# Five edits at the seams between the stages of a graph layer on one core

## The chip, the cores and the metric

The kernel runs on one core of one Trainium2 chip. The metric is the device time of one execution in microseconds (us), as the median of several runs. Engines are called as the profile calls them: PE (TensorE, with PEld for its weight loads), DVE (VectorE), ACT (ScalarE), POOL (GpSimd) and SP (SyncE, which here only issues DMAs).

## The reference

One layer works on 32 graphs of 512 nodes with 256 channels, in float32. In short, with the parts that the kernel's stages answer to:

```python
h = jnp.maximum(_layernorm(x), 0.0)                    # x is (32, 512, 256)
# two convolutions along the nodes, 1 tap and 17 taps, with folded batch norms
c = relu(bn1(conv1d(h^T, conv1_w)))
x_conv = relu(bn2(conv1d(c, conv2_w, pad=8)) + h^T)^T
# message passing with affinities from a 3-wide embedding
s = h @ w_se.T + b_se
A = exp(-dist(s, s)) * adj                              # (32, 512, 512)
msg = relu(h @ w_msg.T + b_msg)
x_nmp = A @ msg
# a GRU cell on [x_conv, x_nmp] and h
gi = concat([x_conv, x_nmp]) @ w_ih.T + b_ih
gh = h @ w_hh.T + b_hh
r, z = sigmoid(gi_r + gh_r), sigmoid(gi_z + gh_z)
n = tanh(gi_n + r * gh_n)
return x + (1 - z) * n + z * h
```

## The kernel before

The 32 graphs go in two groups of 16 (`GB = 16`). Within a group the index `b` below counts from 0 to 15 of that group unless a graph number is given.

**First part** (`first_part`, once per group, L1163). For each graph: `statistics` (mean and variance on DVE, L392 to L397, the power -1/2 on POOL, L398), `normalise` (L400: one instruction for each of the four chunks of 128 nodes, on DVE at L411 or on ACT at L409; the ACT form needs `shift`, which DVE makes at L405), `transpose_h` (eight PE transposes at L419 into two banks, a relu out of each bank at L423, or at L421 on ACT for the second half of the first graph), `conv1` (16 matmuls at L439, an addition on DVE at L442 and a relu on ACT at L443) and `windows_to_freq` (matmuls at L454, copies on ACT at L457), which turns windows of 64 nodes into 80 frequency rows. The 17-tap convolution is later a product per frequency.

In the first group the 17-tap weights are turned into frequency rows beside this: 32 steps of `weights_to_freq` (four matmuls into four banks at L363, four copies out at L371 on DVE and L373 on ACT, and after every second step four DMAs on the SP queue at L377 to a DRAM buffer `wd`). The inner function `between(b)` says how many steps a graph gets: two at b = 0, none at b = 1, then two each, with a third at b = 6 and at b = 11. It also starts other loads, and at b = 6 the step `vectors`, whose POOL instructions (L255 to L267) wait for a DMA. The taps of the next eight input channels come by `load_taps` on the POOL queue at even b (L350, L351).

**Left-over products.** The first group's last four frequency products (`u0` to `u3`, of 40 "units") are done inside the second group's first part. The list `left` (L1440) says at which of five points (`fill`) which of them is prepared (`prepare`: a sum of weights at L470 and a sum of factors at L483, both on POOL) and multiplied (`product`: matmuls at L503, copies at L509 and L510 on ACT, additions at L511 and L512 on DVE). The third entry also holds `*combine.pop(0)`, the load of the gate weights `w_hh` by four DMAs on the POOL queue (L211).

**Nodes** (`nodes`, once per group, L1318). Messages (`message`: matmuls at L558, additions at L560 and L561 on DVE, squares at L564 and relu at L565 on ACT), embedding rows (`features`, L572 to L575), factors (`factors`: two transposes at L580 and L584, a copy at L582 and four masked copies at L587 on ACT), exponents (matmuls at L604, exp on ACT at L610), mask (L593, L614 on DVE), aggregation in seven products (`aggregate7`, L666) and the frequency products. The first two graphs of the list `todo` are set up ahead of the loop.

**Gates**. 16 pairs of graphs: the inverse transform (`inverse`, L874 to L882), 26 products that give r and z (`gates_rz26`, L911, in the order of `PRODUCTS`) and seven for n (`gate_n`, L928). Both sides of the 26 products are sums of blocks; `block_sum` makes the sums of activations, on POOL (L808, L810). For the first pair the order is `FIRST_ORDER`; the one sum that is named `FIRST_ORDER[ahead]`, which is `('t4', 'c')`, goes to DVE.

All of these run under a manual schedule: instructions reach each engine in the order in which the Python code issues them, every engine works its own list in that order, and only semaphores join them. Eight PSUM banks are handed round in turn under the one tag `bank`, so a group of matmuls waits for the copy out of the bank that was taken eight allocations before.

Of the kernel before, what the change touches and what calls it, by code (L numbers as in the profile page):

```python
# [12 lines left out]
AF = mybir.ActivationFunctionType  # L13
# [149 lines left out]
def gnn_layer(  # L163
# [15 lines left out]
    nc = tc.nc  # L179
# [217 lines left out]
        nc.vector.tensor_scalar(rstd, mv[:, :, 1], LN_EPS, None, op0=ALU.add)  # L397
        nc.gpsimd.tensor_tensor(rstd, rstd, minus_half[:, :NC], op=ALU.pow)  # L398

    def normalise(b, by_scalar=False):  # L400
        mv, rstd = STATS.pop(b)
        XN[b] = pools["first"].tile([P, NC, D], FP, tag="xn", name=f"xn_{b}", bufs=2)
        if by_scalar:
            shift = work.tile([P, NC], FP, tag="shift", name=f"shift_{b}")
            nc.vector.scalar_tensor_tensor(shift, mv[:, :, 0], -1.0, rstd, op0=ALU.mult, op1=ALU.mult)  # L405
        for c in range(NC):
            dst, src = by_half(XN[b][:, c, :]), halves(X[b][:, c, :])
            if by_scalar:
                nc.scalar.activation(dst, src, AF.Identity, bias=shift[:, c : c + 1], scale=rstd[:, c : c + 1])  # L409
            else:  # L410
                nc.vector.tensor_scalar(dst, src, mv[:, c, 0:1], rstd[:, c : c + 1], op0=ALU.subtract, op1=ALU.mult)  # L411
        del X[b]
# [130 lines left out]

    SQ = {}

    def message(b, halves=range(2)):
        if 0 in halves:
            ST[b] = pools["nodes"].tile([P, NC, NS + 1], FP, tag="st", name=f"st_{b}", bufs=2)
            MSG[b] = pools["nodes"].tile([P, NC, D], FP, tag="msg", name=f"msg_{b}", bufs=3)
        hq = HQ[b]  # L550
        h = NC // 2
        for c0 in (h * k for k in halves):
            m = MSG[b][:, c0 : c0 + h, :]
            for j in range(h):
                c = c0 + j
                p = bank(f"pm_{b}_{c}")
                for ic in range(DC):
                    nc.tensor.matmul(p[:, : D + NS], hq[:, ic, c * P : (c + 1) * P], wmsg[:, ic, :],  # L558
                                     start=(ic == 0), stop=(ic == DC - 1))
                nc.vector.tensor_add(ST[b][:, c, :NS], p[:, D : D + NS], bmsg[:, D:])  # L560
                nc.vector.tensor_add(m[:, j, :], p[:, :D], bmsg[:, :D])  # L561
            if c0 > 0:
                SQ[b] = work.tile([P, NC, NS], FP, tag="sq", name=f"sq_{b}")
                nc.scalar.activation(SQ[b], ST[b][:, :, :NS], AF.Square)  # L564
            nc.scalar.activation(m, m, AF.Relu)  # L565
        if 1 in halves:
            del HQ[b]

# [222 lines left out]
    def block_sum(p, name, part):  # L791
        if name in BLOCK_SUMS:
            x, op, y = BLOCK_SUMS[name]
            dst, x, y = (operand(p, v, part) for v in (name, x, y))
            op = ALU.add if op == "+" else ALU.subtract
        else:
            rows = list(PAIR_SUMS)

            def whole(v):
                if isinstance(v, int):  # L800
                    return CP[p][:, v] if part == "c" else HN[p][:, :, v]
                return TNC[0][:, rows.index(v)] if part == "c" else TN[0][:, rows.index(v)]

            (x, y), op = PAIR_SUMS[name], ALU.subtract
            dst, x, y = whole(name), whole(x), whole(y)
            if part == "hn":
                for k in range(2):
                    nc.gpsimd.tensor_tensor(dst[:, k], x[:, k], y[:, k], op=op)  # L808
                return
        (nc.vector if (p, name, part) == (0, *FIRST_ORDER[ahead]) else nc.gpsimd).tensor_tensor(dst, x, y, op=op)  # L810

    def sums_ahead(p, part):
        for name in SUMS_AHEAD:
# [349 lines left out]
    def first_part(g, freq, between, left=()):  # L1163


        b0, b1 = g * GB, (g + 1) * GB
        for b in range(b0, b0 + 3):
            if b not in X and (g == 0 or b == b0):
                load_x(b)
        if g == 0:  # L1170
            t = XN[b0] = pools["first"].tile([P, NC, D], FP, tag="xn", name="rows", bufs=2)
            ones, diags = t[:, 0, :P], t[:, 1:3, :].rearrange("p i (c m) -> p i c m", m=P)
            nc.vector.memset(ones, 1.0)

            for _ in range(10):
                nc.tensor.matmul(row1[1][:, :P], ident, fr.rearrange("p g c k -> p (g c k)"), start=True, stop=True)
            batch_norm("bn1", scale1, shift1, nc.gpsimd)
            bn1_row(0, scale1, ones, diags)
            bn1_row(1, shift1, ones, diags)
        if b0 not in STATS:  # L1180
            statistics(b0)
        normalise(b0)
        if g == 0:
            scale_w1()
            shift_w1()
        left = list(left)

        def fill():
            for step in left.pop(0) if left else ():
                step()  # L1190

        if g > 0:
            place_h1(b0)
            load_x(b0 + 1)
            fill()
            load_x(b0 + 2)
        transpose_h(b0)
        statistics(b0 + 1)
        fill()
        normalise(b0 + 1, g > 0)  # L1200
        if g > 0:
            statistics(b0 + 2)
        fill()
        for b in range(b0, b1):
            if b + 3 < b1:
                load_x(b + 3, nc.sync if b < 3 else nc.gpsimd)
            if b == b0:
                conv1(b)
                one, two = between(0) if g == 0 else ([], [])
                for step in one:  # L1210
                    step()
                fill()
                if g == 0:
                    transpose_h(b + 1)
                    statistics(b + 2)
                    normalise(b + 2)
                else:
                    normalise(b + 2)
                    transpose_h(b + 1)
                fill()  # L1220
                xf, last_two = freq(g), two
                continue
            if g == 0:

                slots = last_two if b == b0 + 1 else between(b - b0)

                def slot():
                    for step in slots.pop(0) if slots else ():
                        step()

                if b == b0 + 1:
                    between(b - b0)
                    conv1(b)
                    slot()
                if b == b0 + 2:
                    slot()
                if b == b1 - 1:
                    by_chunks(b - 1)
                    load_h(b0)
                if b + 2 < b1:  # L1240
                    statistics(b + 2)
                if b + 1 < b1:
                    transpose_h(b + 1)
                if b > b0 + 2:
                    slot()
                if b + 2 < b1:
                    normalise(b + 2)
                if b > b0 + 1:
                    conv1(b)
                    slot()  # L1250
                if b == b1 - 1:
                    by_chunks(b)
                windows_to_freq(b - 1, xf)
                slot()
                continue
            if b == b1 - 1:
                by_chunks(b - 1)
                load_h(b0)
            if b + 2 < b1:
                statistics(b + 2)  # L1260
            if b + 1 < b1:
                transpose_h(b + 1)
            if b + 2 < b1:
                normalise(b + 2)
            one, two = between(b - b0)
            conv1(b)
            for step in one:
                step()
            windows_to_freq(b - 1, xf)
            for step in two:  # L1270
                step()
        if g > 0:
            by_chunks(b1 - 1)
        windows_to_freq(b1 - 1, xf)
        return xf
# [8 lines left out]
    with tc.tile_pool(name="freq", bufs=1) as fpool:  # L1284
# [3 lines left out]
        with phase("first", "gen"):  # L1288
# [13 lines left out]
            def between(b):  # L1302
                if 1 <= b <= len(load_weights):
                    load_weights[b - 1]()

                n = (2, 0, *(3 if b in (6, 11) else 2 for b in range(2, GB)))[b]
                mine = [[steps.pop(0)] for _ in range(n)]
                if b % 2 == 0 and b // 2 + 1 < QI // PI:
                    mine[b > 0].insert(0, partial(load_taps, gen, b // 2 + 1))
# [8 lines left out]
        def nodes(g, xf, units, last, following=()):  # L1318
# [29 lines left out]
            features(todo[0])  # L1348
            for step in message_sums(todo[0]):
                step()  # L1350
            message(todo[1], [0])
            factors(todo[0])
            by_chunks(todo[2])
            message(todo[1], [1])
            features(todo[1])
# [67 lines left out]
        with phase("pw", "ahead"):  # L1423
# [3 lines left out]
            with phase("first", "sums"):  # L1427
                combine = combine_weights()

                def between(b):  # L1430

                    if b == GB - 3:
# [6 lines left out]
                pw, (u0, u1, u2, u3) = pools["pw"], range(UNITS - LEFT, UNITS)  # L1439
                left = [[partial(load_unit, 0, u2, pools["sums"]), partial(prepare, pw, 0, u1, xf)],  # L1440
                        [partial(product, pw, 0, u0, xf), partial(prepare, pw, 0, u2, xf)],
                        [partial(product, pw, 0, u1, xf), partial(load_unit, 0, u3), *combine.pop(0)],
                        [partial(prepare, pw, 0, u3, xf), partial(product, pw, 0, u2, xf)],
                        [partial(product, pw, 0, u3, xf)]]
                prepare(pw, 0, u0, xf)
                with tc.manual_schedule():
                    xf = first_part(1, freq_tile, between, left)
# [95 lines left out]
```

## Time and profile before

| what | us |
|---|---|
| time, median of 3 runs | 1734.13 (1733.61 to 1734.86) |
| the profiled execution's own time | 1737.52 |
| its span, first to last instruction | 1735.7 |
| PE busy in it | 1718.5 (99%) |
| DVE busy | 1300.2 (75%) |
| POOL busy | 1086.8 (63%) |
| ACT busy | 692.6 (40%) |
| first part of group 0 | about 0 to 161 |
| nodes of group 0 | about 161 to 425 |
| left-over products and first part of group 1 | about 425 to 544 |
| nodes of group 1 | about 544 to 822 |
| gates | about 822 to 1736 |

How to read it: times in the views are microseconds from the span's start. A row of the timeline has the start, the length, the engine, the line, the operation, what it writes and reads, and in brackets how long the engine had been idle and what released it. Rows that merge several instructions give the length from the first start to the last end. A busy PE is not a PE at full speed: matmuls are pipelined, and one that is held up between two matmuls of a group only makes the group longer.

### The profile page before, as it was taken

To read this page: it belongs to the slowest core of one execution; us is meant where nothing else is said; L and a number is where in the kernel's file an instruction comes from. 1 tells how busy PE (TensorE), PEld (TensorE's weight loads), DVE (VectorE), ACT (ScalarE), POOL (GpSimd) and SP (SyncE) were. 2 spreads that over 40 slices of the span, in tenths; PEclk is the share of its full clock that TensorE was granted. 3 is DMA by queue.
4 is the path that set the end of the run, shared out by engine and by line. 5 is a ranking of instruction groups with operands and counts; after the bars stand their busy time and mean duration, and the time that the engine had idled before them with its cause. 6 is when DMAs were issued, how large, how long until landed. Compare 5 with 4: busy or idle time off the path is not lost.

```text
span 1735.7 us, 24321 instructions
## 1 busy us (share of the span) xinstructions
PE 1718.5 (99%) x7920; PEld 1323.0 (76%) x7920; DVE 1300.2 (75%) x2599; ACT 692.6 (40%) x1671; POOL 1086.8 (63%) x1071
## 2 busy tenths in 40 slices
PE   9999999999999999999999999999999999999998
PEld 6667888888898888886877787777877787778754
DVE  7785877777995667766587778777887788777867
ACT  4557555553446555554313232223223231323221
POOL 3341787777654677777767556765666556755551
PEclk9999999999999999999999999999999999999999
DMA  9988978975777988788523453245423552345323
GB/s 256 296 282 250 272 219 240 262 223 180 256 268 211 265 245 257 219 251 297 150 74 75 107 127 107 70 79 128 118 71 67 128 128 76 76 104 127 106 59 73
DMA packets 311682, 295.08 MB, mean 170 GB/s; under 512 B 147436, under 2 KB 241164, under 8 KB 311172
## 3 DMA queue, kind: packets, MB, share of 16 engines
q1 hardware_dynamic: 301588, 265.17, 55.7%
q0 software_dynamic: 6960, 26.65, 4.8%
q10 hardware_dynamic: 3008, 1.72, 0.3%
q8 instruction: 63, 1.03, 0.2%
q14 instruction: 63, 0.52, 0.1%
HBM read 194.31 MB, written 99.16 MB: 169 GB/s over the span
## 4 chain that ended last, share of the span: by engine, by line
PE 93%; DVE 2%; POOL 2%; DMA 1%; ACT 1%; SPq 1%; issue 1%; POOLq 0%; DVEq 0%; ACTq 0%
PE pg L911 29%; PE pn L928 17%; PE py L503 11%; PE pn L666 10%; PE pm L558 6%; PE pc L439 5%; PE px L454 3%; PE pc L874 3%; PE pd L604 2%; PE pw L363 2%; PE phT L419 1%; PE pg L928 1%; PE pz L928 1%; PE pc L877 1%; POOL tn L808 0%
## 5 line engine op out<-in xcount | busy, mean ns | idle before, releaser
L470 POOL TENSOR_TENSOR wsum<-wt 128x512 f32<-128x512 f32 x66 | 94.5, 1432 | 99.6 <-DMA wt<-wd 65.7
L503 PE MATMUL py<-wt,xf 128*128 128x256 f32 x640 | 154.2, 384 | 0.0
L911 PE MATMUL pg<-te,sw 128*128 128x256 f32 x600 | 154.0, 379 | 0.0
L902 ACT ACTIVATE rz<-rz,brz 128x256 f32<-128x256 f32 x180 | 86.4, 504 | 149.2 <-DVE rz L917 149.2
L503 PEld LDWEIGHTS py<-wt,xf 128*128 128x128 f32 x640 | 117.1, 190 | 34.9 <-issue 20.5
L911 PEld LDWEIGHTS pg<-te,sw 128*128 128x128 f32 x600 | 114.0, 190 | 15.5
L911 PE MATMUL pg<-hn,sw 128*128 128x256 f32 x480 | 123.2, 379 | 0.0
L911 PE MATMUL pg<-tn,sw 128*128 128x256 f32 x480 | 123.2, 379 | 0.0
L614 DVE TENSOR_TENSOR A<-A,at 128x512 f32<-128x512 f32 x124 | 116.2, 975 | 6.3 <-ACT A L610 2.7
L928 PE MATMUL pn<-tn,sw_n 128*128 128x512 f32 x256 | 120.3, 592 | 0.0
L439 PE MATMUL pc<-w,hT 128*128 128x256 f32 x512 | 119.2, 386 | 0.8 <-DVE hT L423 0.8
L1073 ACT ACTIVATE pn<-nt,vech 128x512 f32<-128x512 f32 x45 | 31.1, 692 | 217.8 <-DVE nt L1070 138.5
L558 PE MATMUL pm<-wmsg,hq 128*128 128x259 f32 x512 | 117.3, 381 | 0.0
L439 PEld LDWEIGHTS pc<-w,hT 128*128 128x128 f32 x512 | 95.9, 192 | 24.9 <-issue 8.0
L808 POOL TENSOR_TENSOR tn<-hn 128x512 f32<-128x512 f32 x64 | 86.2, 1367 | 35.7 <-PE pn L928 35.6
L558 PEld LDWEIGHTS pm<-wmsg,hq 128*128 128x128 f32 x512 | 96.6, 190 | 14.6
L911 PEld LDWEIGHTS pg<-hn,sw 128*128 128x128 f32 x480 | 91.1, 190 | 18.3 <-PE pn L928 3.3
L911 PEld LDWEIGHTS pg<-tn,sw 128*128 128x128 f32 x480 | 91.2, 190 | 12.4
L917 DVE TENSOR_TENSOR ct<-pg,ct 128x256 f32<-128x256 f32 x180 | 74.6, 415 | 32.9 <-PE pg L911 23.7
L398 POOL TENSOR_TENSOR rstd<-rstd,minus_half 128x4 f32<-128x4 f32 x32 | 33.3, 1042 | 103.0 <-DVE rstd L397 98.5
L928 PEld LDWEIGHTS pn<-tn,sw_n 128*128 128x128 f32 x256 | 48.6, 190 | 61.2 <-issue 50.5
L928 PE MATMUL pn<-hn,sw_n 128*128 128x512 f32 x192 | 90.3, 592 | 0.0
(232 smaller groups left out, 4385.4 us busy)
## 6 DMA issues: line engine op xcount, KB each, us to landing
wt<-wd SPq DMA_DIRECT2D x80, 512.0 KB, 6.3
adj<-in_adj_dram SPq DMA_DIRECT2D x128, 256.0 KB, 5.9
wd<-wst SPq DMA_DIRECT2D x64, 320.0 KB, 5.5
yd<-y SPq DMA_DIRECT2D x76, 256.0 KB, 5.0
hd<-hT SPq DMA_DIRECT2D x32, 512.0 KB, 4.4
nd<-nmp SPq DMA_DIRECT2D x32, 512.0 KB, 2.9
xb<-in_x_dram SPq DMA_DIRECT2D x128, 128.0 KB, 6.0
out_dram<-xb SPq DMA_DIRECT2D x122, 128.0 KB, 2.8
```

The costliest lines, as they stand in the source:

```text
L439: nc.tensor.matmul(p[:, j, :], HT[b][:, ic, c * P : (c + 1) * P], w1[:, ic, :], start=(ic == 0), stop=(ic == DC - 1))
L454: nc.tensor.matmul(p[:, j * 2 * L : (j + 1) * 2 * L], H1[b][:, c0 + j, ic * P : (ic + 1) * P], fwd, start=True, stop=True)
L470: nc.gpsimd.tensor_tensor(t, WT[g, u][:, 0], WT[g, u][:, 1], op=ALU.add)
L503: nc.tensor.matmul(dst, v[:, ic, :], w[:, ic, :], start=(ic == 0), stop=(ic == DC - 1))
L558: nc.tensor.matmul(p[:, : D + NS], hq[:, ic, c * P : (c + 1) * P], wmsg[:, ic, :], start=(ic == 0), stop=(ic == DC - 1))
L614: nc.vector.tensor_mul(A[b][:, mc, :], EXP.pop((b, mc)), AT.pop((b, mc)))
L666: nc.tensor.matmul(bk, left[:, k, :], right[:, k, :], start=(first and k == 0), stop=(k == 1), skip_group_check=True)
L808: nc.gpsimd.tensor_tensor(dst[:, k], x[:, k], y[:, k], op=op)
L902: nc.scalar.activation(at(dst), at(src), AF.Sigmoid, bias=brz[:, o : o + 1], scale=sign)
L911: nc.tensor.matmul(bk, SW["hk"][:, k, s, :], c if k == 2 else hn[:, k], start=(onto is None and k == 0), stop=(k == K3 - 1), skip_group_ch ...
L917: nc.vector.tensor_tensor(at(dst), at(x), at(y), op=op)
L928: nc.tensor.matmul(bk[:, t], weight(q, k, o), terms[k][q][:, t], start=(first and i == 0), stop=(i == len(ks) - 1), skip_group_check=True)
```

## The change

Five places are edited.

1. **First normalisation.** `normalise` takes the set of chunks that ACT does. For the first graph of group 0 these are chunks 2 and 3; before, DVE did all four. `shift` is made on DVE ahead of them. Elsewhere nothing changes (all on DVE, or all on ACT for the second graph of group 1).
2. **Third weight transforms.** The third step of `weights_to_freq` is at b = 12 and b = 14 instead of b = 6 and b = 11.
3. **First factors' copies.** In `nodes`, ahead of the loop, the relu of the first half of the second graph's message is issued on ACT after the copies of the first graph's `factors` instead of before them.
4. **Gate weights' first load.** The load of `w_hh` on the POOL queue moves from the third to the fifth entry of `left`, behind the last of the four products.
5. **A sum of the first gates.** Of the first pair, `('r5', 'c')`, the entry of `FIRST_ORDER` after `('t4', 'c')`, goes to DVE too.

```diff
-    def normalise(b, by_scalar=False):
+    def normalise(b, by_scalar=()):
         ...
         for c in range(NC):
             dst, src = by_half(XN[b][:, c, :]), halves(X[b][:, c, :])
-            if by_scalar:
+            if c in by_scalar:
                 nc.scalar.activation(dst, src, AF.Identity, bias=shift[:, c : c + 1], scale=rstd[:, c : c + 1])
             else:
                 nc.vector.tensor_scalar(dst, src, mv[:, c, 0:1], rstd[:, c : c + 1], op0=ALU.subtract, op1=ALU.mult)
...
-    def message(b, halves=range(2)):
+    def message(b, halves=range(2), later=None):
...
-            nc.scalar.activation(m, m, AF.Relu)
+            relu = partial(nc.scalar.activation, m, m, AF.Relu)
+            if later is None:
+                relu()
+            else:
+                later.append(relu)
...
-        (nc.vector if (p, name, part) == (0, *FIRST_ORDER[ahead]) else nc.gpsimd).tensor_tensor(dst, x, y, op=op)
+        (nc.vector if p == 0 and (name, part) in FIRST_ORDER[ahead : ahead + 2] else nc.gpsimd).tensor_tensor(dst, x, y, op=op)
...
-        normalise(b0)
+        normalise(b0, range(2, NC) if g == 0 else ())
...
-        normalise(b0 + 1, g > 0)
+        normalise(b0 + 1, range(NC) if g > 0 else ())
...
-                n = (2, 0, *(3 if b in (6, 11) else 2 for b in range(2, GB)))[b]
+                n = (2, 0, *(3 if b in (12, 14) else 2 for b in range(2, GB)))[b]
...
-            message(todo[1], [0])
+            relus = []
+            message(todo[1], [0], relus)
             factors(todo[0])
+            for relu in relus:
+                relu()
             by_chunks(todo[2])
...
-                        [partial(product, pw, 0, u1, xf), partial(load_unit, 0, u3), *combine.pop(0)],
+                        [partial(product, pw, 0, u1, xf), partial(load_unit, 0, u3)],
                         [partial(prepare, pw, 0, u3, xf), partial(product, pw, 0, u2, xf)],
-                        [partial(product, pw, 0, u3, xf)]]
+                        [partial(product, pw, 0, u3, xf), *combine.pop(0)]]
```

## The prediction

> **What bounds the kernel now.** I read the page first, then PE's waits, then the timeline around each edited place, then the granted clock in short windows.
>
> ```profile
> PE 1718.5 (99%) x7920; PEld 1323.0 (76%) x7920; DVE 1300.2 (75%) x2599; ACT 692.6 (40%) x1671; POOL 1086.8 (63%) x1071
> ```
>
> PE is the bound nearly everywhere, so an edit is worth what it takes out of PE's stream and nothing else. These are PE's waits, in us, times, longest; left out are the very first one, one on hT (0.8), one on POOL's sums at 420 and two of 0.3:
>
> ```profile
> PE py L503 <- POOL both L483: 2.0, 1, 2.0
> ...
> PE psl L580 <- ACT fl L573: 0.7, 2, 0.3
> PE phT L419 <- DVE xn L411: 0.6, 1, 0.6
> PE pd L604 <- DVE msg L561: 0.5, 1, 0.5
> PE pd L604 <- ACT sr L587: 0.5, 1, 0.5
> PE px L454 <- DVE h L442: 0.4, 1, 0.4
> PE pg L911 <- POOL tnc L810: 0.3, 1, 0.3
> PE pw L363 <- ACT wst L373: 0.3, 1, 0.3
> ```
>
> All together they come to 9 us, and each of the five edits stands at one of them: both (2.0) is edit 4, xn at the start edit 1, pd (twice) edit 3, pw and px edit 2, tnc edit 5. The windows show one more loss that is no wait; the column before the last two is the granted clock.
>
> ```profile
> 70.00:74.00 4.00, 3.28 (x17) 1.85 (x16) 1.81 (x4) 3.61 (x9) 3.34 (x7) 1.00 0.89 138
> 74.00:78.00 4.00, 4.00 (x19) 1.90 (x17) 3.96 (x13) 1.34 (x5) 1.10 (x2) 0.55 0.99 326
> 78.00:82.00 4.00, 4.00 (x12) 3.27 (x13) 2.45 (x7) 1.51 (x3) 0.74 (x1) 0.60 1.00 323
> ```
>
> At 74 to 82 us the clock falls to about half, and the same three groups (transposes, weight step, conv1) that took 67.62 - 61.98 = 5.64 us one graph earlier take 83.16 - 74.19 = 8.97: **3.33 us**. Until the tail there is no other fall. The profiled execution took 1737.52, the median is 1734.13: 3.39 apart, nearly this number. I take it that the timed runs have no such fall, so 1737.52 - 3.33 = 1734.19 stands for the median, and I sum against that.
>
> **Edit 1, first normalisation.** DVE now does four chunks at 7.23 to 8.61 (period 0.325), then the weight scaling (0.74), then hT from 9.19; conv1 starts at 9.93. New: `shift` on DVE, two chunks (0.65), scaling to 8.71. `shift` is 128x4: the row of the same width, rstd L397, takes 0.17 (about 0.1 of issue time); the only `shift` in the trace takes 1.22, but beside a POOL addition (434.46 to 435.72), and here POOL is idle. ACT starts at 7.45; its chunk is 2.08/4 = 0.52 (L409), so it ends at 8.49 instead of DVE's 8.61. The last transpose of the first bank then ends at 8.80 and hT starts at 8.85 instead of 9.19: **-0.34**. ACT's shift row copy (0.37) moves behind its chunks to 8.86, ahead of its half of hT, which is ready at 9.3, and it is first read at 14.1. DVE is the pace until about 34 (it waits only for rstd), so the gain stays only if the next statistics can start: their x, issued at 3.58, landed 5.7 later, at 9.28; they would start at 9.45 instead of 9.79. Ends: `shift` at 1.22 gives +0.7; both waits gone, -0.6.
>
> **Edit 2, third weight transforms.** At b = 6 the third step meets ACT's copies (0.51 apart), which free the eight banks in turn:
>
> ```profile
> 72.14 2.12 PE L363 MATMUL pw<-w2p,taps 17*80 17x512 f32 x8 [0.32 <-ACT wst L373]
> 74.19 1.82 PE L419 MATMUL phT<-ident,xn 128*128 128x128 f32 x8
> ```
>
> Without it the next transposes take the same banks at 72.14, so the 0.32 stays, and so does px's 0.40 before it, which `vectors` makes (POOL waits for its DMA until 65.04, rstd ends at 68.34). But a weight bank takes 0.21 of loading and then idles 0.27 twice before the next copy; a bank of transposes takes 0.97/2 = 0.48 and idles 0.03. Saved: 2 x 0.24 = **0.48**. The step itself (1.03 of PE, four copies of 0.51 on ACT or 0.68 on DVE) only moves. At b = 11 the step costs 0.16 + 0.22 in the two weight groups after it (1.19 and 1.25 from start to start instead of 1.03); I give b = 12 the same and b = 14 nothing, as DVE has no more statistics there and idles 2.01. What moves along: from b = 7 to 14 each step's copies come later and the SP stores of `wd` go with them, two sets at b = 14, the last one still at b = 15; at b = 8 and 10 `load_taps` on POOL waits for the second step instead of the first, and behind it on POOL stand the x loads and rstd. The same order already runs at b = 4: POOL idles 4.70 there, rstd ends at 55.8 instead of about 54.5, PE waits for nothing. Ends: -0.86 (both new places free) to -0.1 (both cost 0.38).
>
> **Edit 3, copies.** ACT idles 0.78 ahead of the relu, which waits for DVE's second addition, while the factors are ready:
>
> ```profile
> 167.01 0.63 ACT L565 ACTIVATE msg<-msg 128x512 f32<-128x512 f32 x1 [0.78 <-ACT fr L575]
> 167.55 0.25 ACT L582 COPY sl<-psl 128x128 f32<-128x128 f32 x1
> 167.69 1.14 ACT L587 ACTIVATE sr<-psr,mask 128x128 f32<-128x128 f32 x4
> ```
>
> In the loop the sl copy starts 0.31 after its transpose (806.63, 806.94), so at 166.24 + 0.31 = 166.55; sr ends at 167.83 instead of 168.83, before PE's messages end at 168.33, and pd's wait (0.5) goes. But PE then waits for fl of the second graph, which sits behind relu and hq copies on ACT: ACT's whole list comes 167.01 - 166.55 = 0.46 earlier, and that is all PE gets: **-0.46**, and in group 1 550.47 - 550.00 = **-0.47**. The fl wait of 0.34 stays or grows. Nobody near waits for the delayed relu. Ends: 0 to -1.7 (all four waits).
>
> **Edit 4, first load.** POOL issues the four loads ahead of u3's two sums:
>
> ```profile
> 439.41 2.19 POOL L211 DMA_DIRECT2D w<-in_w_hhT_dram  x4
> ...
> 442.29 3.00 DVE L411 TENSOR_SCALAR xn<-x,mv,rstd 128x256 f32<-128x256 f32 x4
> 442.41 1.27 POOL L470 TENSOR_TENSOR wsum<-wt 128x512 f32<-128x512 f32 x1
> 443.63 0.79 POOL L483 TENSOR_TENSOR both<-xf 128x256 f32<-128x256 f32 x1
> 444.47 1.13 PE L503 MATMUL py<-wsum,both 128*128 128x256 f32 x4 [1.97 <-POOL both L483]
> ```
>
> Without them x is issued at 439.46 and the sums run 440.3 to 442.3 (u3's weights landed at 430.77 + 8.9 = 439.7). PE needs them at 442.35: the 1.97 goes, PE ends at 443.2. Next late is DVE: xn starts at 442.29 as now (behind the additions of u2), but free of POOL's sums it takes 1.40 as at 12.78 instead of 3.00, hT (1.27) follows, and conv1, which needs both halves of hT, runs as if begun at 444.47 instead of 446.31: **-1.84**. Moved: the four DMAs go to 442.3 to 444.5, ahead of the next x load, which stays at 444.4; they land 4.8 later, by 449.3, and are first read 1.84 earlier than now, at 454.5. Ends: 0 (xn still 3.00 long) to -1.97.
>
> The nearest row for loads beside xn is at 12.70: five POOL loads took 0.53 to 0.75 each, as elsewhere, and xn 1.40. [...]
>
> **Edit 5, a sum.** The sum takes 0.69 on DVE (827.43, t4) and DVE idles 5.76 after that; its input is relu'd at 828.27, so it ends at 829.0, and PE's wait of **0.33** at 833.10 goes. POOL's list gets 1.27 shorter; the next sum it owes, E5, ends near 832.8 and is read at 835.5. Beside t4's sum a POOL instruction takes 1.60 instead of 1.26 (827.65); a second such 0.34 leaves E5 2 us early. Ends: 0 to -0.33.
>
> **Sum.** 0.34 + 0.48 + 0.46 + 0.47 + 1.84 + 0.33 = 3.92 us; after each place PE is continuous again, and the one wait between (420.51, POOL ts, 0.78) follows a POOL list that PE itself started at 400.15. 1734.13 - 3.92 = **1730.2**. A change of 0.2% is 3.47 us, about what a measurement of this kernel can tell from none: below 1730.66 is faster.
>
> **Rivals.** (a) The fall of the clock is in the timed runs too, and goes with the three crowded weight groups before it: 1730.2 - 3.33 = 1726.9. For: it follows that place. Against: the 3.39 that agrees with 3.33. What calls a fall up is open: waits of 0.40 and 0.32 came before this one, and 1.97 at 442.5 before none. [...] (c) Slower: the moved weight steps call up clock falls at their new places. Half speed costs 0.5 us per us; from 3.92/0.5 = 7.8 us of it (this fall was 6.7) the change is slower than before, from 14.8 us by over 0.2%: three falls, 1730.2 + 10 = 1740.2. Against: b = 11 has the same order now, at full clock. (d) An edit does nothing: if the copies only move the wait to fl, 1731.1.
>
> **How the numbers follow.** Forecast 0.56, of which 0.48 below 1730.66; (a) 0.20; (b) 0.12; (d) 0.05; (c) 0.07. Faster 0.48 + 0.20 = 0.68; same 0.08 + 0.12 + 0.05 = 0.25; slower 0.07. The range goes from (a) with 0.4 of the better ends, 1726.5, to (b) with 0.2 more, 1732.2; (c) is left out.
>
> **What would show it.** Right: no wait of py for both; xn at the third graph of group 1 near 1.4; pd without a wait and fl's still there; no tnc wait; pc of the first graph at 9.6; one wait of 0.3 at 72 on phT, no pw. Wrong: xn still at 3 us; a half clock in the windows of b = 12 to 15; first waits on DMA at 454; the profiled time still about 3.4 above the median without a fall.

## The result, and the profile after

| | us |
|---|---|
| before, median of 22 runs | 1734.76 (1733.34 to 1742.89) |
| after, median of 22 runs | 1732.55 (1730.92 to 1737.7) |
| ratio after to before | 0.9984 (95% interval 0.9976 to 0.9992) |
| after once more, another session | 1733.55 against 1736.19, ratio 0.998 (0.9969 to 0.999) |
| profiled execution after: own time, span | 1733.51, 1731.7 |

The change is faster, by 2.2 us where 3.9 were forecast: less than the 0.2% (3.5 us) that the prediction had set for "faster", but the interval leaves 1 out. The median lies 0.35 above the upper end of the range, and the kernel before came out 0.63 above the 1734.13 from which the forecast was subtracted; taken as a difference, 2.2 lies inside the range (1.9 to 7.6). The page's first part shows PE as full as before:

```profile
PE 1716.3 (99%) x7920; PEld 1324.1 (76%) x7920; DVE 1301.9 (75%) x2599; ACT 692.8 (40%) x1673; POOL 1084.7 (63%) x1070
```

PE's waits after the change (us, times, longest), complete but for the very first:

```profile
PE psl L584 <- ACT fl L577: 1.6, 2, 0.8
...
PE pc L439 <- DVE hT L423: 1.2, 2, 0.9
PE phT L419 <- DVE xn L411: 0.9, 2, 0.7
PE pn L670 <- POOL ts L645: 0.8, 1, 0.8
PE phT L419 <- ACT wst L373: 0.6, 2, 0.3
PE px L454 <- ACT wst L373: 0.3, 1, 0.3
```

The waits that the edits aimed at are gone: `both`, `pd` twice, `tnc`, `pw`. In their place `fl` went from 0.7 to 1.6, and two waits behind DVE are larger, hT (0.9 at 16.2) and xn (0.7 at 454.2). The windows at 70 to 82 (PE's busy time first, the granted clock third from the end) have no fall:

```profile
70.00:74.00 4.00, 3.68 (x26) 2.63 (x24) 3.97 (x14) 3.95 (x10) 3.92 (x8) 1.00 0.88 142
74.00:78.00 4.00, 4.00 (x19) 2.96 (x16) 3.28 (x8) 1.68 (x4) 1.31 (x2) 1.00 0.98 336
78.00:82.00 4.00, 4.00 (x31) 3.13 (x31) 3.14 (x11) 3.10 (x8) 0.04 (x1) 1.00 1.02 366
```

**Edit 2's old place**, from the timeline: the 0.32 stays on the transposes and the step is gone, as forecast.

```profile
71.80 1.14 PE L419 MATMUL phT<-ident,xn 128*128 128x128 f32 x8 [0.32 <-ACT wst L373]
72.87 1.62 PE L363 MATMUL pw<-w2p,taps 17*80 17x512 f32 x8
```

**Edit 3.** The copies run 1.17 ahead of the relu, `pd` waits for nothing, and the next graph's `psl` waits 0.76 where it waited 0.33:

```profile
162.66 0.27 ACT L586 COPY sl<-psl 128x128 f32<-128x128 f32 x1 [0.31 <-PE psl L584]
162.82 1.15 ACT L591 ACTIVATE sr<-psr,mask 128x128 f32<-128x128 f32 x4
163.83 0.65 ACT L1359 ACTIVATE msg<-msg 128x512 f32<-128x512 f32 x1
164.42 1.14 PE L608 MATMUL pd<-sr,sl 32*128 32x512 f32 x8
...
166.32 0.33 PE L584 MATMUL psl<-ident,fl 128*128 128x128 f32 x1 [0.76 <-ACT fl L577]
```

**Edit 4.** xn takes 1.37 and py waits for nothing; but x of graph 20 goes out at 441.19, right behind the four loads, its statistics wait 2.54 for it, and PE pays at 454 and 455.6. In the kernel before, x of graph 20 and its statistics were:

```profile
444.37 0.83 POOL L215 DMA_DIRECT2D x<-in_x_dram  x1
...
453.34 1.39 DVE L392 BATCH_NORM_STATS2 stats<-x 128x6 f32<-128x256 f32 x4
```

and after the change:

```profile
438.91 2.29 POOL L211 DMA_DIRECT2D w<-in_w_hhT_dram  x4
438.98 1.37 DVE L411 TENSOR_SCALAR xn<-x,mv,rstd 128x256 f32<-128x256 f32 x4
439.05 1.10 PE L503 MATMUL py<-wsum,both 128*128 128x256 f32 x4
...
441.09 3.79 PE L439 MATMUL pc<-w,hT 128*128 128x256 f32 x16
441.19 0.77 POOL L215 DMA_DIRECT2D x<-in_x_dram  x1
...
450.42 1.40 DVE L392 BATCH_NORM_STATS2 stats<-x 128x6 f32<-128x256 f32 x4 [2.54 <-DMA x<-in_x_dram]
...
454.23 1.17 PE L419 MATMUL phT<-ident,xn 128*128 128x128 f32 x3 [0.66 <-DVE xn L411]
```

**Edit 1.** conv1 of graph 0 starts at 9.39 instead of 9.93 (0.29 of this because the last of x of graph 0 was there earlier, at 4.23 instead of 4.52). Then the statistics of graph 1 wait for x, and conv1 of graph 1 starts at 16.21, later than before. The kernel before:

```profile
9.79 1.39 DVE L392 BATCH_NORM_STATS2 stats<-x 128x6 f32<-128x256 f32 x4
...
16.04 3.89 PE L439 MATMUL pc<-w,hT 128*128 128x256 f32 x16 [0.34 <-DVE hT L423]
```

and after the change:

```profile
9.39 3.72 PE L439 MATMUL pc<-w,hT 128*128 128x256 f32 x16 [0.35 <-DVE hT L423]
9.95 1.41 DVE L392 BATCH_NORM_STATS2 stats<-x 128x6 f32<-128x256 f32 x4 [0.61 <-DMA x<-in_x_dram]
...
16.21 2.16 PE L439 MATMUL pc<-w,hT 128*128 128x256 f32 x8 [0.89 <-DVE hT L423]
```

**Edit 5.** The second sum on DVE takes 1.48, the first 0.68; the second ends 3.5 before DVE is wanted again:

```profile
823.82 0.68 DVE L814 TENSOR_TENSOR tnc<-cp 128x512 f32<-128x512 f32 x1
824.69 1.48 DVE L814 TENSOR_TENSOR tnc<-cp,tnc 128x512 f32<-128x512 f32 x1 [0.19 <-ACT cp L886]
829.68 0.42 DVE L921 TENSOR_TENSOR ct<-ct,pg 128x256 f32<-128x256 f32 x1 [3.51 <-PE pg L915]
```

So all five did what they say at their own place, and three of them had given something back a few graphs later. The experiments ask whether that giving back belongs to the edits or to this one execution.

### The profile page after: what moved, and what is told of

Read it like the earlier page. It is cut to its first block, busy times and chain, and to the rows that moved or that the text cites. A ratio compares the mean times of both kernels' runs of the same rounds, so it can differ in the third digit from the quotient of the medians.

```text
span 1731.7 us, 24322 instructions
## 1 busy us (share of the span) xinstructions
PE 1716.3 (99%) x7920; PEld 1324.1 (76%) x7920; DVE 1301.9 (75%) x2599; ACT 692.8 (40%) x1673; POOL 1084.7 (63%) x1070
## 3 DMA queue, kind: packets, MB, share of 16 engines
q8 instruction: 63, 1.03, 0.2%
## 4 chain that ended last, share of the span: by engine, by line
PE 93%; DVE 3%; DMA 2%; POOL 1%; SPq 1%; ACT 0%; issue 0%; DVEq 0%; POOLq 0%; ACTq 0%
PE pg L915 29%; PE pn L932 17%; PE py L503 11%; PE pn L670 10%; PE pm L558 6%; PE pc L439 5%; PE pc L878 4%; PE px L454 3%; PE pd L608 2%; PE pw L363 1%; PE phT L419 1%; PE pg L932 1%; PE pz L932 1%; PE pc L881 1%; PE pn L653 1%; DMA x<-in_x_dram 1%
## 5 line engine op out<-in xcount | busy, mean ns | idle before, releaser
L439 PE MATMUL pc<-w,hT 128*128 128x256 f32 x512 | 117.8, 383 | 1.2 <-DVE hT L423 1.2
L439 PEld LDWEIGHTS pc<-w,hT 128*128 128x128 f32 x512 | 94.8, 190 | 24.2 <-issue 6.4
L932 PEld LDWEIGHTS pn<-tn,sw_n 128*128 128x128 f32 x256 | 48.7, 190 | 61.1 <-issue 50.6
```

The costliest lines, as they stand in the source:

```text
L439: nc.tensor.matmul(p[:, j, :], HT[b][:, ic, c * P : (c + 1) * P], w1[:, ic, :], start=(ic == 0), stop=(ic == DC - 1))
L932: nc.tensor.matmul(bk[:, t], weight(q, k, o), terms[k][q][:, t], start=(first and i == 0), stop=(i == len(ks) - 1), skip_group_check=True)
```

## The experiments

Most edits are worth less than the scatter of single times (a standard deviation of 0.8 to 1.8 us, and up to 3.0 where the clock falls in some executions), so the traces decide: PE's stream has fixed anchors, the starts of conv1 (L439) of each graph and of each graph's exponents (`pd`, L604). The table has the time between anchors for every trace of the case. "1" is the start of conv1 of graph 1; "6 to 7", "10 to 11", "6 to 15", "16 to 20" are from one graph's conv1 to the other's; "pd" is from the second to the fifth graph's exponents in group 0. A free graph takes 8.95 in group 0, and a third step adds 1.03. An asterisk marks a trace with the clock's fall at 74 to 82.

| kernel | edits | 1 | 6 to 7 | 10 to 11 | 6 to 15 | 16 to 20 | pd |
|---|---|---|---|---|---|---|---|
| before | none | 16.04 | 13.91* | 8.96 | 87.88* | 32.28 | 47.98 |
| e1_alone | 1 | 15.57 | 13.97* | 8.95 | 88.21* | 32.12 | 47.79 |
| e2_alone | 2 | 16.13 | 11.35 | 10.19 | 85.41 | 32.61 | 48.65 |
| e4_alone | 4 | 16.03 | 11.93 | 8.95 | 84.26 | 30.53 | 48.03 |
| after | all | 16.21 | 10.25 | 9.68 | 83.79 | 32.38 | 49.02 |
| after_again | all | 16.38 | 10.50 | 9.78 | 84.14 | 30.19 | 49.27 |
| f1_x1_first | all, x(1) first | 15.90 | 10.88 | 9.32 | 84.26 | 32.03 | 48.54 |
| f2_steps_7_14 | all, steps 7, 14 | 16.44 | 10.16 | 8.95 | 82.97 | 30.60 | 48.49 |
| f4_x_first | all, x(20) first | 17.26 | 10.57 | 10.40 | 84.83 | 30.54 | 47.99 |
| v14 | all, vectors at 14 | 15.89 | 8.96 | 9.62 | 82.44 | 30.50 | 48.80 |
| best | all, these four | 15.82 | 8.96 | 8.96 | 81.78 | 30.51 | 48.93 |
| best_again | the same | 16.02 | 8.95 | 8.95 | 81.77 | 30.22 | 49.43 |
| best_7_11 | the same, steps 7, 11 | 15.82 | 9.87 | 8.95 | 83.38 | 31.53 | 48.62 |
| c6_vectors | none, vectors at 14 | 15.99 | 10.14 | 8.96 | 82.48 | 32.76 | 47.78 |

### Edit 4, alone and with x first

The edit of `e4_alone` is edit 4's two lines in the kernel before. `f4_x_first` puts the loads behind x of graph 20:

```diff
-                        [partial(product, pw, 0, u3, xf), *combine.pop(0)]]
+                        [partial(product, pw, 0, u3, xf)],
+                        combine.pop(0)]
...
                 load_x(b + 3, nc.sync if b < 3 else nc.gpsimd)
+            if b == b0 + 1:
+                fill()
```

> The kernel before with edit 4 alone. My theory: the 1.9 us that edit 4 takes out at the left-over products is given back three graphs later, because the load of x for graph 20 now stands on the POOL queue behind the four loads of the gate weights and lands late. So the third graph's xn takes about 1.4 instead of 3.0 and conv1 of graph 17 starts about 1.9 earlier than in the kernel before, measured from the last PE work ahead of the place; then the statistics of graph 20 wait 1.5 to 2.6 for x, and from conv1 of graph 19 on PE is at most 0.4 ahead. Time within 0.5 of the kernel before. Rival: the slow landing (9.2 us instead of 4.7) was an accident of one execution; then the statistics do not wait, PE stays 1.9 ahead and the time is 1.9 lower.

> The changed kernel, with the four loads of the gate weights issued after the load of x for graph 20 instead of ahead of it. My theory: x of graph 20 is issued at about 438.9 and lands before its statistics want it (no wait over 0.3 where the changed kernel has 2.54), PE keeps the 1.9 from conv1 of graph 19 on, and the time is 1.5 to 2.0 below the changed kernel's. Rival: the transfers only share the DMA engines, whichever is issued first: then the statistics of graph 20 or 21, or POOL's first sum of gate weights, wait for about as long as they did, and the time is that of the changed kernel within 0.5.

`e4_alone`: 1733.86 (ratio 0.9995, 0.9983 to 1.0006). conv1 of graph 17 came as forecast, but no statistics waited: graphs 16 to 20 took 30.53 and PE kept 1.75. So the theory missed and its rival held, in this execution. `f4_x_first`: 1732.76 (0.9984, 0.9975 to 0.9993), not measurably below the changed kernel; its trace shows x first and no wait 9 us later:

```profile
439.78 0.78 POOL L215 DMA_DIRECT2D x<-in_x_dram  x1
440.56 2.15 POOL L211 DMA_DIRECT2D w<-in_w_hhT_dram  x4
...
448.76 1.39 DVE L392 BATCH_NORM_STATS2 stats<-x 128x6 f32<-128x256 f32 x4
```

Together with the later traces the answer is a spread. Of six traces with the gate weights ahead, x of graph 20 was late in four (waits of 2.54, 2.04, 1.15 and 1.11; it landed 9.2, 9.2, 7.8 and 7.8 after its issue) and not in two, where DVE asked for it 7.4 after the issue. From conv1 of graph 17 to that of graph 20 these six took 21.70, 21.20, 20.21, 19.81, 19.69 and 19.68. With x ahead, in four traces, its statistics never waited, and the same stretch took 19.98 and three times 19.69. The loss is real, 0 to 2.0 us an execution and 0.7 on average. But the kernel before has a loss of the same kind. There the four loads stand ahead of x of graph 19: in the four traces without edit 4 it landed 6.0, 6.2, 7.0 and 7.1 after its issue (4.0 to 5.0 with edit 4), its statistics waited 0.50, 0.68, 1.46 and 1.51, and graphs 17 to 20 took 19.67, 19.85, 20.62 and 20.68. So edit 4 hands a late load from graph 19 to graph 20, and against the kernel before that costs 0.7 - 0.5 = 0.2 on average.

### Edit 2, alone and with the steps at 7 and 14

```diff
-                n = (2, 0, *(3 if b in (12, 14) else 2 for b in range(2, GB)))[b]
+                n = (2, 0, *(3 if b in (7, 14) else 2 for b in range(2, GB)))[b]
```

> The kernel before with edit 2 alone. My theory: the half clock at 74 to 82 us does not appear; conv1 of graph 7 is 0.5 to 0.9 ahead without counting the clock; then the loads that POOL issues at b = 8 wait for the second weight step of the graph instead of the first, the loads of x for graphs 11 and 12 bunch up, the statistics of graph 12 wait 1 to 2.6 us for x, and 0.5 to 0.8 of PE is lost between b = 10 and b = 11. Time within 0.5 of the kernel before. Rival one: the fall of the clock is in the usual execution of the kernel before too: 3 to 4 us lower. Rival two: the loss at b = 10 came from edit 1 (a shifted DVE), then no wait there and the time is 0.5 to 0.9 lower.

> The changed kernel, with the third weight steps at b = 7 and 14 instead of 12 and 14. My theory: the loads at b = 8, 10 and 12 then wait for the first step of their graph, as in the kernel before; POOL issues them at once after it, the statistics of graph 12 wait under 0.3 for x, and PE is 0.5 to 0.8 further ahead after b = 11 than in the changed kernel. Rival: a third step costs 0.4 to 0.5 wherever the copies on ACT and DVE are in step with PE, so that b = 7 pays what b = 10 saves, or the clock falls again there: within 0.3 of the changed kernel, or 3 above it.

`e2_alone`: 1735.62 (0.9996, 0.9987 to 1.0005). No fall of the clock; graph 11 came 10.19 after graph 10, 1.24 late, behind a wait of 2.99 for x of graph 12. `f2_steps_7_14`: 1731.95 (0.9981, 0.9973 to 0.999); graph 11 in 8.95, and graphs 6 to 15 in 82.97. The table has the loss at graph 11 in six of six traces with the steps at 12 and 14 (0.4 to 1.45, mean 0.88), and in none of the eight others. The rows of POOL and DVE show how. Of the two loads of x in each view the first is that of graph 12, whose statistics are the last row. The kernel before:

```profile
88.95 2.90 POOL L350 DMA_DIRECT2D w2p<-in_w2T_dram  x4 [0.29 <-PE pw L363]
92.45 0.80 POOL L215 DMA_DIRECT2D x<-in_x_dram  x1
...
103.50 1.39 DVE L392 BATCH_NORM_STATS2 stats<-x 128x6 f32<-128x256 f32 x4
```

The changed kernel:

```profile
88.54 2.17 POOL L350 DMA_DIRECT2D w2p<-in_w2T_dram  x4 [5.54 <-PE pw L363]
91.31 0.80 POOL L215 DMA_DIRECT2D x<-in_x_dram  x1
93.13 0.80 POOL L215 DMA_DIRECT2D x<-in_x_dram  x1
100.40 1.40 DVE L392 BATCH_NORM_STATS2 stats<-x 128x6 f32<-128x256 f32 x4 [2.48 <-DMA x<-in_x_dram]
```

and the kernel with the steps at 7 and 14:

```profile
87.02 3.08 POOL L350 DMA_DIRECT2D w2p<-in_w2T_dram  x4
90.70 0.80 POOL L215 DMA_DIRECT2D x<-in_x_dram  x1
94.27 0.80 POOL L215 DMA_DIRECT2D x<-in_x_dram  x1
100.03 1.39 DVE L392 BATCH_NORM_STATS2 stats<-x 128x6 f32<-128x256 f32 x4
```

With the third step gone from b = 6, `load_taps` at b = 8 waits for the second step of its graph (5.54 idle), and x of graph 12, the first load behind the taps, goes out late with it: 10.0 ahead of conv1 of graph 10 in the six traces with the loss, 11.9 to 13.9 ahead in the other eight. DVE wants it 6.6 after its issue in the six (9.0 to 11.1 in the others); it landed 8.7 to 9.8 after its issue in the six and 7.5 to 9.1 in the others, so the time ahead differs more than the landing. In each of the six, PE's loss is DVE's wait less 1.75 (waits of 2.11 to 3.20, losses of 0.36 to 1.44): that much slack stands between the two. The loads of graphs 12 and 13 (the expectation calls them 11 and 12) also move together, 1.8 apart instead of 3.6 to 5.1, but it is the first of them that is waited for. Which kernels had the loss follows from the steps alone: a third step ahead of b = 8 removes it.

### Edit 1, alone and with x of graph 1 first

```diff
+            load_x(1)
             load_w1()
-            load_x(1)
```

> The kernel before with edit 1 alone. My theory: conv1 of graph 0 starts 0.3 to 0.5 earlier (9.4 to 9.6 instead of 9.92), but the next thing that DVE needs, x of graph 1, lands somewhere between 9.3 and 11.0 (six traces so far), so the statistics of graph 1 wait 0.1 to 1.4 for it and conv1 of graph 1 starts at 16.0 to 17.3, not before the 16.04 of the kernel before. Rival, the prediction's own: x is there at 9.3, conv1 of graph 1 starts at 15.7 and PE keeps 0.34. The time cannot tell these apart (under 0.5); the trace can.

> The changed kernel with the load of x for graph 1 issued ahead of the four loads of w1. My theory: it is issued at 1.7 instead of 3.6, so it is there before 9.2, the statistics of graph 1 start by 9.4 without a wait, conv1 of graph 1 starts at 15.5 to 15.8 and conv1 of graph 6 at 63.5 to 63.8 (64.0 in the kernel before, 64.2 to 65.2 with edit 1). Rival: what is moved behind it is missed: DVE's scaling of w1 waits for w1 and conv1 of graph 0 starts up to 1.5 late, or x of graph 1 shares the engines with the rest of x of graph 0 and delays that.

`e1_alone`: 1736.05 (0.9997, 0.9988 to 1.0007). Here the theory missed, because x of graph 1 was early:

```profile
9.31 1.40 DVE L392 BATCH_NORM_STATS2 stats<-x 128x6 f32<-128x256 f32 x4
...
15.57 3.67 PE L439 MATMUL pc<-w,hT 128*128 128x256 f32 x15 [0.35 <-DVE hT L423]
```

The six traces with edit 1 and the load in its old place have waits of 0, 0, 0.39, 0.61, 0.78 and 1.41 there, and conv1 of graph 1 between 15.57 and 17.26, mean 16.29; without edit 1 it is 16.05 (four traces, 15.99 to 16.13). On the chain itself, from the start of the last three statistics instructions of graph 0 to its conv1, edit 1 is worth the same everywhere: 5.15 to 5.17 with it and 5.39 to 5.41 without. `f1_x1_first`: 1733.19 (0.9986, 0.9975 to 0.9997); no wait for x of graph 1, in this kernel and three later ones, and conv1 of graph 1 at 15.82 to 16.02, mean 15.89, somewhat later than expected. The rival was also right in part: w1 comes later, and where x of graph 0 was early (4.31, 4.33) the scaling of w1 held conv1 up, to 5.45 and 5.58 on that chain.

### The vectors, and what the clock follows

```diff
         load_vectors,
-        vectors,
+        lambda: None,
         scale_embedding,
         partial(nc.sync.dma_start, back, nc.inline_tensor(back_np, name="dft_back").ap()),
+        *[lambda: None] * 5,
+        vectors,
```

`v14` has this in the changed kernel, `c6_vectors` in the kernel before.

> The changed kernel with the step of the vectors (POOL's wait for its DMA and eight small instructions) moved from b = 6 to b = 14. In the traces so far PE takes 10.3 to 11.4 from conv1 of graph 6 to conv1 of graph 7 without a third weight step there, against 8.95 in a free graph. My theory: this is POOL's wait for the vectors, behind which rstd of graph 8 stands; moved, the step from graph 6 to 7 takes 8.9 to 9.6, the waits of phT and px at 68 to 72 are gone, and PE keeps 1 to 2 us. Rival: x of graph 8, whose statistics waited 0.5 to 2.2 for its load in every trace, is as late, and 10 to 11 stays.

> The kernel before with the step of the vectors moved from b = 6 to b = 14; the third weight step stays at b = 6. So far executions with the third step and the vectors both at b = 6 had a granted clock of 0.997 or less over the whole span in 32 of 83, and kernels without the third step there in 3 of 81. My theory: the fall of the clock follows a weight step that meets waits of PE at the same graph, so without the waits (graph 6 to 7 in 10.0 to 10.4 instead of 11.93) at most 1 execution in 10 has the low clock, and the median is 1732.5 to 1733.5. Rival: three weight steps at b = 6 call the fall up by themselves: 3 to 5 executions in 10 at 0.997 or less, and a median of 1734 to 1735.

`v14`: 1731.78 (0.9971, 0.9959 to 0.9982). Graph 7 follows graph 6 in 8.96, with no wait of PE:

```profile
68.53 2.44 PE L456 MATMUL px<-fwd,h 128*128 128x160 f32 x16
70.81 1.04 PE L421 MATMUL phT<-ident,xn 128*128 128x128 f32 x8
71.78 1.10 PE L365 MATMUL pw<-w2p,taps 17*80 17x512 f32 x8
```

So 1.2 to 2.4 us were lost at b = 6 in every trace with the vectors there and no fall of the clock, and edit 2, which works at this very place, could not reach them. `c6_vectors`: 1733.95 (0.9986, 0.9977 to 0.9995), somewhat above what was expected; graph 7 in 10.14, that is 8.95 + 1.03 + 0.16. One execution of twelve had a granted clock of 0.997 or less, and at 1734.25 it was no longer than the others.

Counted over all timed executions that list their clock: with a third step and the vectors at b = 6, 43 of 120 had 0.997 or less over the whole span (of the kernel before, 37 of 98, one outlier left out); without the third step there, 4 of 108. The kernel before took 1738.4 on average in its 37, and 1735.2 in the other 61. Each of the two traces that fell in this class, of `before` and of `e1_alone`, has the fall at the same place:

```profile
74.00:78.00 4.00, 4.00 (x19) 1.99 (x18) 3.97 (x14) 1.62 (x4) 1.19 (x2) 0.57 1.00 359
78.00:82.00 4.00, 4.00 (x12) 3.19 (x12) 2.47 (x6) 1.16 (x3) 0.65 (x1) 0.57 0.94 281
```

Without the third step the low clock is all but gone. Without the waits it came once in twelve, against 7 of 23 for the kernel before in the same session: twelve executions point the same way, but do not settle it. It is not the waits alone: in `e2_alone` PE is idle for 1.28 of the 4 us at 70 to 74, more than the 0.72 of before, and the clock stays at 1.00. What calls the fall up is open.

### All four places together

`best` is the changed kernel with the edits of `f1_x1_first`, `f2_steps_7_14`, `f4_x_first` and `v14`; `best_7_11` has its third steps at 7 and 11.

> The changed kernel with four places rearranged: the load of x for graph 1 ahead of w1, the third weight steps at b = 7 and 14, the step of the vectors at b = 14, and the gate weights behind the load of x for graph 20. My theory: each place where the change's gain was lost is free, so conv1 of graph 1 starts near 15.7, graph 11 follows graph 10 in 8.95, graph 7 follows graph 6 in 8.9 to 9.6, graph 20 has no wait; PE ends 2 to 3 us ahead of the kernel with the third steps at 7 and 14, and the time is 1728 to 1730. Rival: transfers that no longer wait meet others: some load lands late in its turn, and the time stays at 1731 to 1732.

> The changed kernel once more, to see how its places scatter from one execution to the next, on the chip of the kernel below. My theory: graph 11 comes 9.6 to 10.4 after graph 10 as in five of five traces, graph 19 comes 6.5 to 8.4 after graph 18, graph 1 starts at 15.6 to 17.3; the median is 1732 to 1733.5. Rival: the losses of the first trace were accidents, and this one is free of them at 1730.5.

> The kernel with four places rearranged, once more, beside the changed kernel. My theory: no wait at graphs 1, 7, 11 and 20, and 2 to 3 us below the changed kernel (1729.5 to 1730.8). Rival: its first runs were lucky, under 1 us below the changed kernel.

> The kernel with four places rearranged, but with the third weight steps at b = 7 and 11 instead of 7 and 14, so that no step ends later than in the kernel before. In nine traces with a third step at b = 14 PE takes 31.8 to 33.2 (mean 32.55) from the second to the fourth graph's exponents of group 0, in four without it 31.6 to 31.8. My theory: the step at b = 14 pushes the last stores of the weights, behind which the loads of the weights and of the second graph's adjacency stand on SP's queue, so DVE waits longer for the adjacency. With 7 and 11 those two graphs take 31.5 to 31.9, DVE's wait for the adjacency near 175 falls from 3.5 to 1.4 to 2.2; the step costs 0.4 to 0.5 more at b = 11 than at b = 14, so the time is 0.2 to 0.6 lower than with 7 and 14 (1729.6 to 1730.2). Rival: edit 3's earlier factors are what the adjacency cannot follow; then it stays at 32.3 to 33.2 and the time is 0.4 higher.

`best`: 1730.46 (0.9962, 0.995 to 0.9975). Again, beside the changed kernel: 1730.02 (0.9961, 0.9946 to 0.9977) against 1733.55. The first is between its theory and its rival, the second as expected. The kernel beats both others, by 6.2 and 3.5 us of the medians, and the waits at graphs 1, 7, 11 and 20 are gone in both its traces. `after_again` shows the losses at graphs 1, 11 and 20 once more (DVE waiting 0.39, 2.57 and 1.11 for x; at graph 20 PE lost only 0.13 of it), so they belong to the change.

`best_7_11`: 1730.83 (0.9969, 0.996 to 0.9979). DVE's wait for the adjacency of the second graph, from the timeline of `e4_alone`:

```profile
175.94 1.30 DVE L593 STREAM_TRANSPOSE at<-adj 128x512 f32<-128x512 f32 x2 [1.62 <-DMA adj<-in_adj_dram]
```

and of `best_7_11` (3.53 in `best_again`):

```profile
176.38 1.30 DVE L599 STREAM_TRANSPOSE at<-adj 128x512 f32<-128x512 f32 x2 [3.98 <-DMA adj<-in_adj_dram]
```

From the second to the fourth graph it took 31.57, as the theory has it, but DVE's wait was 3.98 and 0.83 went a graph later, so the column "pd" stays at 48.62. Neither theory is shown. This trace also lost 0.9 from graph 6 to 7, where DVE waited 2.65 for x of graph 8 (1.03 and 1.29 in the two traces of `best`), and 1.0 from graph 16 to 17, beside waits of 2.42 and 2.23 for x of graphs 17 and 18. The column "pd" is 47.8 to 48.0 in the four traces with neither edit 3 nor a step at b = 14, 48.65 with that step alone, 48.62 with edit 3 and no such step (`best_7_11`), and 48.0 to 49.4 (mean 48.8) with both. So group 0 gives back 0.9 on average with both, and between 0.1 and 1.5 in single traces. Two things stand there: with edit 3 DVE waits 0.3 to 1.1 for the adjacency of the first graph in eight of nine traces, and in none of five without it; and in `e2_alone`, which has no such wait, DVE's two products with that adjacency at 171.45 took 1.51 and 1.21, beside POOL's sums, where such a product takes 0.68 alone. How much each costs PE, and which edit makes the adjacency late, stays open.

## Why the prediction was right or wrong

**The bound** was read rightly. What a stall on PE gave, the next PE work got; what was lost again came, at graphs 1, 12 and 20, through loads that DVE waits for.

**Edit 1, -0.34.** Measured -0.25 on the chain to conv1 of graph 0, and then +0.24 on average at graph 1 (16.29 against 16.05). The failed step is "they would start at 9.45 instead of 9.79": it took one landing, 9.28, as a fixed time, 0.17 ahead of its new reader. In the ten traces that issue it there, the load lands anywhere from 7.7 to 11.0.

**Edit 2, -0.48.** From graph 6 to 15 five traces took 83.79 to 85.41, mean 84.49, against 84.26 in the one trace with neither edit 2 nor a fall: +0.2. By parts: -0.2 from graph 6 to 7 (10.71 on average against 11.93 less the 1.03 of the step), about -0.5 from graph 11 to 15, where two steps now cost less than the one at b = 11 did, and +0.88. Failed step: "The same order already runs at b = 4: [...] PE waits for nothing", which priced the move of `load_taps` at nothing. It was paid with those 0.88. And the trace of before held the warning: at b = 4 the loads of x go out at 53.99 and 55.80, again 1.8 apart, and the first, of graph 8, is late:

```profile
61.51 1.40 DVE L392 BATCH_NORM_STATS2 stats<-x 128x6 f32<-128x256 f32 x4 [0.72 <-DMA x<-in_x_dram]
```

That wait cost PE nothing, being inside the slack: in `v14`, `best` and `best_again`, without the vectors at this place, waits of 1.28, 1.29 and 1.03 there cost PE nothing either, and 2.65 in `best_7_11` cost 0.9, again the wait less 1.75. But the same load, issued at the same distance from PE, was waited for 0.49 to 2.65 over the 14 traces. One execution in which a late load is covered is no price for it.

**Edit 3, -0.46 and -0.47.** Measured -0.46 and -0.44, with the `fl` wait growing as forecast. Group 1 keeps it: from the second graph's exponents to the gates PE takes 261.98 or 261.99 in all 14 traces. In group 0 about 0.8 is lost again (the column "pd" is 48.7 on average in the six traces of the changed kernel and its single variations, 47.9 in the four with neither edit 3 nor a step at b = 14). The sentence "after each place PE is continuous again" is what failed: it looked at PE's waits and not at DVE, which in the kernel before waits 2.76 for the adjacency soon after. That the adjacency is the cause is not shown.

**Edit 4, -1.84.** From graph 16 to 17 it is -1.6 on average (10.66 in six traces against 12.24 in four), with xn at 1.37 or 1.38 in all six, beside the four loads. The upper end of the range, 1732.2, and the 0.12 of (b) take xn to stay near 3.00 there; no run shows that, and that the median came near that end is chance. The 1.97 that the forecast took out was the longest of four: `py` waited 1.62, 1.34 and 1.43 in the other traces without edit 4. To graph 20 -1.4 (31.04 against 32.44). Failed step: "ahead of the next x load, which stays at 444.4". Its time was an effect of the sums that stood ahead of it on POOL, and went with them; I gave the four loads a cover and never asked for the cover of the load behind them. As graph 19's x lost that place in the queue, the net price is about 0.2, as said above. The sign that I had named, waits at 454, appeared, but for x and not for the gate weights. POOL's issue of the four loads took 2.29 beside xn (438.98 to 440.35) and 2.19 in the kernel before, apart from it.

**Edit 5, -0.33.** Measured -0.41 in every trace with it (-0.58 by the second pair, +0.17 by the third).

**The clock.** "I take it that the timed runs have no such fall" held, to judge by their times, for the three runs shown, not for the kernel: 37 executions of 98 show the low clock and take 3.2 us more on average; that they all have the fall at this place is argued from the two traces with a low clock, which do. So rival (a), at 0.20, was partly what happened. Edit 2 removes the crowded place, and with it about 1.2 us of the average. What calls the fall up stays open: in the traces that fell, PE is idle for 0.72 and 0.64 of the 4 us at 70 to 74, and `e2_alone` with 1.28 did not fall.

**The sum.** +0.24 + 0.2 - 0.46 + 0.8 - 0.44 - 1.4 - 0.41 = -1.5 at the full clock. The stretches in it are where the traces differ; from the fifth graph's exponents of group 0 to conv1 of graph 16, for one, PE takes 209.3 in all 14. Executions at the full clock show -1.0 by the medians (1733.55 against 1734.57, one session) and -1.5 by the means. With 1.2 for the fall that makes some -2.2 to -2.7, against -2.2 and -2.6 measured. The sign was right; of the missing 2.4, about 1.6 went to loads of x that came late for DVE (0.6 at edit 1, 0.9 at edit 2, 0.2 at edit 4) and 0.8 was lost in the nodes of group 0, from a cause that is open; smaller misses cancel. About half of what was measured is the clock, an estimate from the counts above, which the forecast had left to a rival.

## What to carry to other kernels

When a stall is taken out, ask which load the next reader needs, how long before its reader it was issued and how far its landings spread; a load that lands just in time is the next bound. Where a step moves, list every DMA that queues behind it on the same engine, and compare for each the time from its issue to its reader, before and after, with the latest landing seen. Here a wait of DVE for x cost PE only what exceeded the slack of 1.75 behind it, so a small covered wait in one execution (0.72) can be a price in another (2.65, which cost 0.9). A single profile with a low clock is worth a second one: whether the fall is rare or comes in four executions of ten decides what the median is.

## What the runs showed of the hardware

- The same load of 512 KB varies much in its landing: x of graph 1, issued at 3.58 in the same order, landed 4.2 to 7.4 us after its issue in ten traces.
- A load of x behind the four loads of the gate weights on the same queue landed 6.0 to 7.1 us (graph 19, four traces) and 6.7 to 9.2 us (graph 20, six traces) after its issue; x of graph 19 without them ahead took 4.0 to 5.0 in ten traces.
- x of graph 12, behind five loads of taps on that queue, landed 8.7 to 9.8 us after its issue with the next x 1.8 behind it (six traces) and 7.5 to 9.1 with the next x 3.6 to 5.1 behind it (eight traces).
- Three kinds of DVE instructions took longer beside POOL's additions: `shift` 1.22 (the kernel before) instead of 0.16 (the changed kernel), the product with the adjacency 1.2 to 1.8 instead of 0.68, the four chunks of xn of graph 18 3.00, 3.13 and 2.19 (`before`, `e1_alone`, `e2_alone`) instead of 1.37 to 1.40.
- The clock's fall came at one place of the program in the two traces that have it (0.50 at 76 to 80 in the kernel before, 0.57 on average at 74 to 82 in `e1_alone`), and not at longer idle times elsewhere (1.28 of 4 us at 70 to 74 in `e2_alone`, 1.97 at 442.5 in the kernel before). A low clock over the whole span came in 37 of 98 executions of the kernel before.
